# The expert layer of a graph network: tiles, order and the last two experts' output changed

## The chip, the cores and the metric

The kernel runs on one core of one Trainium2 chip. The metric is the device time of one execution in microseconds, the median of several runs. A core has a matrix engine (TensorE, in the profile PE, its weight loads PEld), a vector engine (VectorE, DVE), a scalar engine (ScalarE, ACT), GpSimd (POOL) and SyncE (SP). SP and POOL here mainly issue transfers; every transfer runs on the core's 16 DMA engines.

## What is computed

The input is 625 rows x of 1024 values, a list of 20625 edges and the weights of four layers. Each layer adds its result to x, on a layernorm of x: a gated graph layer with 8 relations, a quantized linear layer, a graph convolution, and a mixture of 8 experts. The change lies in the last one, which in the reference is, cut to what matters:

```python
logits = x @ router_w                       # 625 x 8
combine, dispatch = top2_gating(logits, capacity)
expert_in = einsum('nec,nh->ech', dispatch, x)
hmid = silu(einsum('ech,ehf->ecf', expert_in, w1) + b1)
expert_out = einsum('ecf,efh->ech', hmid, w2) + b2
y = einsum('nec,ech->nh', combine, expert_out)
out = x_before + y + 0.1 * (silu(x @ sw1 + sb1) @ sw2 + sb2)
```

Each token goes to its two best experts, an expert takes at most 196 tokens (its slots), and the two gates of a token add up to 1.

## The kernel before, in words

The graph layers take most of the time; they end with the function neighbours (L764), which adds the graph convolution to X[t] for five row tiles of 125 rows, takes the layernorm into th[t] and writes it to the DRAM table tokens. The function router makes the logits. Then VectorE finds each token's two experts and its place in each; the products positions (L883) and fill_slots (L934) turn this into token_i, which row of tokens a slot of an expert takes, and slots, which holds the slot's gate. A slot that no token takes points at spare rows past the 625th.

The shared expert's second product, shared_out (L954), comes next: per row tile and half of the columns two products, two VectorE operations onto X[t], and the finished X[t] is written to the DRAM table total (L971). This is the base of the result.

The expert loop (L982 to L1042) runs over 8 experts in pool tiles of two buffers. For each: POOL gathers the rows of its slots in two halves of 98 (L986), SP loads its row of b2, repeated on 98 partitions (L990), and its weights w1 and w2 (L993, L994, 1024 KB each); TensorE transposes the gathered rows (16 transposes in four groups, L177), ScalarE copies each group out of PSUM (L180); TensorE makes the hidden product (L1002), ScalarE the Silu (L1009); ScalarE scales b2 by the gates (L1017), TensorE makes the output product (L1022), VectorE scales it and adds the scaled b2 (L1029), and POOL adds the 98 rows into total with an indirect transfer that accumulates (L1032). An expert's two accumulating transfers wait until those of the expert before have landed, since both may hit the same row. When all have landed, SP copies total to the output (L1045).

The order on each engine is the one of the program text, moved by a scheduler where nothing forbids it; in_steps (L822) pins TensorE's steps one behind the other up to shared_out, the expert loop is not pinned. The function in_order (L110) chains transfers on SP in the order of the text. Weights live in two pools of four buffers, wts and late; w_chunk (L127) chains only those of wts. PSUM gives the products four banks (mm_tile, L105) and the transposes two.

The pools of the expert loop are opened where gated and tail were closed (L975, L976), so its tiles lie in memory that th, flat and aT held before.

Of the kernel before, what the change touches and what calls it, by code (L numbers as in the profile page):

```python
# [8 lines left out]
F32 = mybir.dt.float32  # L9
BF16 = mybir.dt.bfloat16  # L10
F32R = mybir.dt.float32r
I32 = mybir.dt.int32
# [19 lines left out]
EG = 11  # L32
BEFORE = 4096.0
NE = 8
F = 256
CAP = 196
CP = CAP // 2
# [8 lines left out]
def gnn_ffn_kernel(  # L46
# [58 lines left out]
    def mm_tile():  # L105
        return ps_mm.tile([128, HC], F32, tag="mm", name="mm")
# [17 lines left out]
        spread(queue, t, bass.AP(tensor=v.tensor, offset=v.offset, ap=[[0, P], [1, v.shape[0]]]))  # L124
        return t

    def w_chunk(pool, w, k0, c0, nk=4, cols=HC):  # L127

        t = pool.tile([128, nk, cols], F32, tag="w", name="w")
        d = nc.sync.dma_start(  # L130
            t,
            w[k0 * 128 : (k0 + nk) * 128, c0 : c0 + cols].rearrange("(k p) n -> p k n", p=128),
        )
        if pool is wts:
            in_order(d)
        return t

# [33 lines left out]
    def transposed(oT, c0, v, n, evacuate=None):  # L171

        for g in range(KD // 4):
            ps = ps_tr.tile([128, 4, 128], F32, tag="tr", name="tr")
            for k in range(4):
                f = (4 * g + k) * 128
                nc.tensor.transpose(ps[:, k, :n], v[:, f : f + 128], ident[:n, :n])  # L177
            o = oT[:, 4 * g : 4 * g + 4, c0 : c0 + n]
            if evacuate is None:
                nc.scalar.copy(o, ps[:, :, :n])  # L180
            else:
                evacuate(o, ps[:, :, :n])


    ident = const.tile([128, 128], F32, name="ident")
# [364 lines left out]
    th = []  # L550
    for t in range(NT):
        transposed(uT, t * P, X[t], P)
        th.append(gp.tile([P, D], F32, name=f"th{t}"))
        nc.scalar.activation(th[t], X[t], AF.Tanh)
        for d in spread(nc.sync, X[t], x[t * P : (t + 1) * P, :]):
            in_order(d)
# [60 lines left out]
            nc.gpsimd.tensor_add(X[t], X[t], q_bias_row)  # L617


    aT = cp.tile([P, NT, N], F32, name="aT")  # L620
    with tc.issue_after(pe_last.ins):
        for k in range(NT):
            for j0, j1 in ((0, 4), (4, NT)):
# [116 lines left out]
    def iota(t, pattern, base, channel):  # L740
        nc.gpsimd.iota(
            t,
            pattern=pattern,
            base=base,
            channel_multiplier=channel,
            allow_small_or_imprecise_dtypes=True,
        )
        return t
# [2 lines left out]
    io_cap = iota(mp.tile([P, CAP], F32, name="io_cap"), [[1, CAP]], 0, 0)  # L751
    io_tok = iota(mp.tile([P, NT, NE], F32, name="io_tok"), [[P, NT], [0, NE]], 0, 1)
    io_free = iota(mp.tile([CP, 2, NE], F32, name="io_free"), [[CP, 2], [0, NE]], N, 1)
    ones_b = mp.tile([P, P], BF16, name="ones_b")
    nc.gpsimd.tensor_copy(ones_b, ones)
    tri_b = mp.tile([P, P], BF16, name="tri_b")
# [100 lines left out]
    nc.vector.reciprocal(red, red)  # L857
    nc.vector.tensor_mul(gates, gates, wide(red))

    masks = mp.tile([P, NT, 2, NE], BF16, name="masks")  # L860
    best = [tile2("best0"), tile2("best1")]

    def argmax_mask(i, v):
# [10 lines left out]
    nc.vector.tensor_scalar(rest, masks[:, :, 0, :], -1.0, 1.0, op0=ALU.mult, op1=ALU.add)  # L874
    nc.vector.tensor_mul(rest, rest, gates)
    argmax_mask(1, rest)


    pos_tile = ps_sm.tile([128, HC], F32, tag="sm", name="pos")
    pos_ps = pos_tile[:P, : (NT + 1) * 2 * NE].rearrange("p (t c) -> p t c", t=NT + 1)  # L880
    mflat = masks.rearrange("p t i e -> p t (i e)")

    def positions(_):  # L883
        for t in range(NT + 1):
            for j in range(t):
                last = nc.tensor.matmul(
                    pos_ps[:, t, :], ones_b, mflat[:, j, :], start=(j == 0), stop=(t == NT and j == t - 1)
                )
            if t < NT:
                nc.tensor.matmul(pos_ps[:, t, :], tri_b, mflat[:, t, :], start=(t == 0), stop=True)  # L890
        return last

    in_steps(((positions, None), (shared_hidden, (0, 3 * P, N)), (shared_hidden, (1, 3 * P, N))))
    pos = mp.tile([P, NT + 1, 2, NE], F32, name="posn")
    nc.vector.tensor_copy(pos.rearrange("p t i e -> p t (i e)"), pos_ps)
    taken = mp.tile([P, 1, NE], F32, name="taken")
    nc.vector.tensor_scalar_min(taken, pos[:, NT:, 0, :], float(CAP))
    nc.vector.tensor_add(pos[:, :NT, 1, :], pos[:, :NT, 1, :], taken.to_broadcast(S3))
# [32 lines left out]
    token_i = mp.tile([CP, 2, NE], I32, name="token_i")  # L931
    free = mp.tile([CP, 2, NE], F32, name="free")

    def fill_slots(j):  # L934
        ps = ps_sm.tile([128, HC], F32, tag="sm", name="slots")
        for i in range(2):
            for t in range(NT):
                last = nc.tensor.matmul(
                    ps[:CP, : NE * 3],
                    place[:, i, t, j * CP : (j + 1) * CP],  # L940
                    brings[:, i, t, :, :].rearrange("p e v -> p (e v)"),
                    start=(i == 0 and t == 0),
                    stop=(i == 1 and t == NT - 1),
                )
        nc.vector.tensor_copy(slots[:, j].rearrange("p e v -> p (e v)"), ps[:CP, : NE * 3])
        nc.vector.tensor_scalar(free[:, j], slots[:, j, :, 0], -1.0, 1.0, op0=ALU.mult, op1=ALU.add)
        nc.vector.tensor_mul(free[:, j], free[:, j], io_free[:, j])
        nc.vector.tensor_add(token_i[:, j], free[:, j], slots[:, j, :, 1])
        return last

    sb2_row = row_tile(work, sb2, "row")
# [19 lines left out]
        base.extend(spread(nc.sync, total[t * P : (t + 1) * P, :], X[t]))  # L971
        return last

    in_steps(((fill_slots, 0), (fill_slots, 1), *((shared_out, t) for t in range(NT))))
    gated.close()  # L975
    tail.close()  # L976

    def rows_at(j, e):
        return bass.IndirectOffsetOnAxis(ap=token_i[:, j, e : e + 1], axis=0)

    sent = base + cleared
    with tc.tile_pool(name="xp", bufs=2) as xp:  # L982
        for e in range(NE):
            xe = xp.tile([CP, 2, D], F32, tag="xe", name="xe")
            for j in range(2):
                nc.gpsimd.indirect_dma_start(  # L986
                    out=xe[:, j, :], out_offset=None, in_=tokens, in_offset=rows_at(j, e)
                )
            b2_row = xp.tile([CP, D], F32, tag="b2", name="b2")
            nc.sync.dma_start(  # L990
                b2_row, bass.AP(tensor=b2.tensor, offset=b2.offset + e * D, ap=[[0, CP], [1, D]])
            )
            wa = w_chunk(wts, w1[e], 0, 0, nk=KD, cols=F)  # L993
            wz = w_chunk(late, w2[e], 0, 0, nk=2, cols=D)  # L994
            xeT = xp.tile([128, KD, CAP], F32, tag="xeT", name="xeT")
            for j in range(2):
                transposed(xeT, j * CP, xe[:, j, :], CP)
            he = xp.tile([128, 2, CAP], F32, tag="he", name="he")
            for f in range(2):
                ps = mm_tile()  # L1000
                for k in range(KD):
                    nc.tensor.matmul(  # L1002
                        ps[:, :CAP],
                        wa[:, k, f * 128 : (f + 1) * 128],
                        xeT[:, k, :],
                        start=(k == 0),
                        stop=(k == KD - 1),
                    )
                nc.scalar.activation(  # L1009
                    he[:, f, :], ps[:, :CAP], AF.Silu, bias=b1_sb[:, e, f : f + 1]  # L1010
                )
            ye = xp.tile([CP, 2, D], F32, tag="ye", name="ye")
            earlier, sent = sent, []
            for j in range(2):
                gate_of = slots[:, j, e, 2:3]
                b2g = work.tile([P, D], F32, tag="xn", name="xn")[:CP, :]
                nc.scalar.mul(b2g, b2_row, gate_of)  # L1017
                for h in range(2):
                    hs = slice(h * HC, (h + 1) * HC)
                    ps = mm_tile()  # L1020
                    for f in range(2):
                        nc.tensor.matmul(  # L1022
                            ps[:CP, :],
                            he[:, f, j * CP : (j + 1) * CP],
                            wz[:, f, hs],
                            start=(f == 0),
                            stop=(f == 1),
                        )
                    nc.vector.scalar_tensor_tensor(  # L1029
                        ye[:, j, hs], ps[:CP, :], gate_of, b2g[:, hs], op0=ALU.mult, op1=ALU.add  # L1030
                    )
                d = nc.gpsimd.indirect_dma_start(  # L1032
                    out=total,
                    out_offset=rows_at(j, e),
                    in_=ye[:, j, :],
                    in_offset=None,
                    compute_op=ALU.add,
                )
                for other in sent:
                    tc.declare_no_dep(d.ins, other.ins, reason="a token has one slot of an expert")  # L1040
                after(d, earlier)
                sent.append(d)  # L1042

    flat_out = [v.rearrange("n d -> (n d)").rearrange("(a b) -> a b", a=80) for v in (out, total[:N, :])]
    after(nc.sync.dma_start(*flat_out), sent)  # L1045


# ---- launch: one core; inputs in the reference's types, weights that are contracted over their
# [39 lines left out]
```

## Time and profile before

| What | Value |
|---|---|
| median of 3 runs | 1367.83 us (1367.31 to 1372.51) |
| profiled execution, its own time | 1372.71 us |
| its span on the profile's clock | 1371.0 us |
| TensorE busy | 1302.0 us, 95% |
| VectorE, ScalarE, GpSimd busy | 604.8, 183.4, 511.1 us |
| DMA moved | 178.79 MB, mean 130 GB/s |
| hidden products of the experts, L1002, 256 records | 46.5 us |
| output products of the experts, L1022, 128 records | 56.2 us |
| slot numbers ready (last token_i) | 1200.5 us |
| shared product on TensorE | 1199.55 to 1216.96 us |
| last expert's product ends | about 1352.4 us |

[...] The chain of waits follows the work that ended last back to what released it. The windows give busy time per engine, then the clock granted to TensorE (1.00 is full), then the mean busy share of the DMA engines and what they moved.

### The profile page before, as it was taken

How to read it: one execution, taken by the hardware profiler on the slowest of the kernel's cores; microseconds unless marked ns; L12 is line 12 of the kernel's file. 1: busy time of each engine (PE TensorE's matmuls, PEld its weight loads, DVE VectorE, ACT ScalarE, POOL GpSimd, SP SyncE). 2: the span in 40 equal slices, each digit the busy share in tenths (PEclk: the TensorE clock that was granted, in tenths of full speed). 3: DMA queues.
4: the chain of work that ended last, by engine and by line, in shares of the span. 5: the costliest groups of instructions: out<-in, count | busy, mean ns of one | idle time of the engine just before them, and what ended most of it. 6: DMA issues, size and time to landing. Idle time of an engine off the chain costs nothing. (4 is left out here: it accounts for less than half of the span.)

```text
span 1371.0 us, 10587 instructions
## 1 busy us (share of the span) xinstructions
PE 1302.0 (95%) x4050; PEld 693.5 (51%) x4050; DVE 604.8 (44%) x1042; ACT 183.4 (13%) x335; POOL 511.1 (37%) x262
## 2 busy tenths in 40 slices
PE   6999999999999999999999999899989999969994
PEld 3444444444444444444777777444445445736652
DVE  6942555555555555001555564423358214441121
ACT  1000000000000000001212211300011111212231
POOL 2016888888888888751200000313100000013221
PEclk9999999999999999999999999999999999989997
DMA  8994445545544443349999722412040231168955
GB/s 252 271 248 119 112 110 122 122 113 122 126 110 120 83 92 73 63 96 236 181 235 226 186 70 94 138 47 93 0 138 15 77 123 49 46 187 233 271 96 122
DMA packets 140155, 178.79 MB, mean 130 GB/s; under 512 B 74758, under 2 KB 91517, under 8 KB 137536
## 3 DMA queue, kind: packets, MB, share of 16 engines
q1 hardware_dynamic: 55998, 126.65, 31.9%
q0 software_dynamic: 79968, 36.12, 17.3%
q10 hardware_dynamic: 4134, 15.29, 3.0%
q8 instruction: 34, 0.56, 0.2%
q14 instruction: 21, 0.17, 0.0%
HBM read 139.04 MB, written 41.18 MB: 131 GB/s over the span
## 5 line engine op out<-in xcount | busy, mean ns | idle before, releaser
L224 PE MATMUL mm<-w,xT 128*125 128x512 f32 x1440 | 622.3, 595 | 1.0 <-ACT xT L180 1.0
L363 POOL DMA_INDIRECT table<-hits,idx x165 | 401.6, 2434 | 138.5 <-issue 68.0
L224 PEld LDWEIGHTS mm<-w,xT 128*125 128x125 f32 x1440 | 270.8, 188 | 348.1 <-issue 345.7
L343 DVE SCALAR_TENSOR_TENSOR junk<-kr,key,wm 125x1375 f32<-125x1375 f32 x165 | 272.4, 1651 | 202.1 <-DMA kr<-key_rows 198.2
L432 PE MATMUL mm<-lo,b 125*125 125x512 f32 x400 | 160.9, 402 | 1.9 <-DVE lo L489 1.9
L432 PE MATMUL mm<-hi,b 125*125 125x512 f32 x400 | 159.5, 399 | 0.0
L388 ACT COPY y<-mm 125x512 f32<-125x512 f32 x80 | 46.8, 585 | 544.2 <-PE mm L224 544.2
L986 POOL DMA_INDIRECT xe<-tokens,token_i x16 | 16.1, 1006 | 226.6 <-DMA total<-X 213.2
L446 DVE SCALAR_TENSOR_TENSOR X<-mm,rc,X 125x512 f32<-125x512 f32 x80 | 60.0, 750 | 76.5 <-PE mm L432 76.3
L432 PEld LDWEIGHTS mm<-lo,b 125*125 125x125 f32 x400 | 75.1, 188 | 22.5 <-DVE lo L489 3.8
L432 PEld LDWEIGHTS mm<-hi,b 125*125 125x125 f32 x400 | 75.0, 188 | 18.0
L571 PE MATMUL mm<-w,xT 128*125 128x512 f32 x160 | 73.2, 603 | 0.0
L1029 DVE SCALAR_TENSOR_TENSOR ye<-mm,slots,xn 98x512 f32<-98x512 f32 x32 | 24.0, 751 | 110.8 <-PE mm L1022 110.8
L695 PE MATMUL mm<-w,xT 128*125 128x512 f32 x160 | 70.0, 595 | 1.6 <-ACT xT L180 1.6
L571 PE MATMUL mm<-w,flat 128*125 128x512 f32 x160 | 70.3, 592 | 0.0
L487 ACT CAST hi<-y 125x512 fp32r<-125x512 f32 x80 | 43.3, 617 | 159.4 <-PE mm L432 159.4
L465 POOL DMA_DIRECT2D btot<-table x16 | 17.7, 1157 | 111.5 <-DMA btot<-table 108.9
L1022 PE MATMUL mm<-w,he 128*98 128x512 f32 x128 | 56.2, 592 | 0.0
L1032 POOL DMA_INDIRECT total<-ye,token_i x16 | 24.7, 1541 | 83.2 <-DVE ye L1029 83.2
L426 DVE TENSOR_SCALAR crow<-cn 1x376 f32<-1x376 f32 (+1 forms) x16 | 7.4, 465 | 106.2 <-PE cn L423 106.2
L489 DVE TENSOR_TENSOR lo<-y,hi 125x512 fp32r<-125x512 f32 x80 | 51.4, 681 | 5.4 <-ACT hi L487 5.4
L1002 PE MATMUL mm<-xeT,w 128*128 128x196 f32 x256 | 46.5, 342 | 6.0 <-ACT xeT L180 6.0
(168 smaller groups left out, 842.1 us busy)
## 6 DMA issues: line engine op xcount, KB each, us to landing
w<-in_L_gnn_weight_dram SPq DMA_DIRECT2D x32, 1024.0 KB
w<-in_L_ffn_w_dram SPq DMA_DIRECT2D x16, 1024.0 KB
table<-zero SPq DMA_DIRECT2D x4, 3054.0 KB
yd<-y ACTq DMA_DIRECT2D x10, 1120.0 KB
y<-yd SPq DMA_DIRECT2D x10, 1120.0 KB
b<-table SPq DMA_DIRECT2D x8, 1367.2 KB
btot<-table POOLq DMA_DIRECT2D x8, 1367.2 KB, 19.1
kr<-key_rows POOLq DMA_DIRECT2D x15, 671.4 KB, 9.3
```

The costliest lines, as they stand in the source:

```text
L224: last = nc.tensor.matmul(ps[:P, :], xT[:, k, t * P : (t + 1) * P], ch[k // 4][:, k % 4, :], start=(k == 0), stop=(k == KD - 1),)
L343: d = nc.vector.scalar_tensor_tensor(junk, kr, key[:, c : c + 1], wm[:, (EG - 1 - j) * P : (2 * EG - 1 - j) * P], op0=ALU.is_equal, op1=AL ...
L363: d = nc.gpsimd.indirect_dma_start(out=table, out_offset=bass.IndirectOffsetOnAxis(ap=idx[:, c : c + 1], axis=0), in_=hits[:, c : c + 1], ...
L388: evac = nc.scalar.copy(y[:, t, :], ps)
L432: last = nc.tensor.matmul(ps[:P, :], lhs, part, start=(k == 0 and part is y[k][0]), stop=(k == NT - 1 and part is y[k][-1]),)
L446: added = nc.vector.scalar_tensor_tensor(X[t][:, hs], ps[:P, :], rc[:, r, t : t + 1], X[t][:, hs], op0=ALU.mult, op1=ALU.add,)
L487: behind(nc.scalar.copy(hi, y[:, k, :]), act_last)
L489: nc.vector.tensor_sub(lo, y[:, k, :], hi.bitcast(F32))
L571: last = nc.tensor.matmul(ps[:P, :], lhs[:, k % KD, ts], gate_w[h][k // 4][:, k % 4, :], start=(k == 0), stop=(k == 2 * KD - 1),)
L695: last = nc.tensor.matmul(ps[:P, :], xT[:, k, t * P : (t + 1) * P], gcn_w[h][k // 4][:, k % 4, :], start=(k == 0), stop=(k == KD - 1),)
L1002: nc.tensor.matmul(ps[:, :CAP], wa[:, k, f * 128 : (f + 1) * 128], xeT[:, k, :], start=(k == 0), stop=(k == KD - 1),)
L1022: nc.tensor.matmul(ps[:CP, :], he[:, f, j * CP : (j + 1) * CP], wz[:, f, hs], start=(f == 0), stop=(f == 1),)
```

## The change

Eight experts as before, with the same products. What differs:

- Expert tiles lie in memory that is idle by then: the gathered rows in th0 to th3 (two experts), the transposed rows in flat, the expert output and b2 in the first three quarters of aT (even experts) and btot (odd experts), the Silu's output in th4. No pools are opened.
- All steps of TensorE are pinned: transposes of expert e+1, turn(e + 1), stand between the hidden product and the output product of expert e.
- POOL issues the gathers of experts 0 and 1 ahead of everything, those of e+2 after the hidden product of e in the text.
- b2, w1 and w2 of an expert are chained on SP in this order (chain=True).
- For experts 6 and 7 a second set of row numbers, out_i, is made: a free slot points not at a spare row but at a token that is not routed to this expert (it adds zero there). These two experts accumulate straight into the output, after total has been copied to it; the copy waits for experts 0 to 5. The row numbers need two more columns in the positions (others), ten comparisons on VectorE (find_others) and 20 small bf16 products among the shared ones (fill_others).

```diff
+NL = 2
-    def w_chunk(pool, w, k0, c0, nk=4, cols=HC):
+    def w_chunk(pool, w, k0, c0, nk=4, cols=HC, chain=False):
...
-        if pool is wts:
+        if pool is wts or chain:
             in_order(d)
...
+    nc.vector.tensor_add(others, masks[:, :, 0, NE - NL :], masks[:, :, 1, NE - NL :])
+    nc.vector.tensor_scalar(others, others, -1.0, 1.0, op0=ALU.mult, op1=ALU.add)
...
+    def find_others():
+
+        nc.vector.tensor_scalar(before, others, -float(N), float(N), op0=ALU.mult, op1=ALU.add)
+        nc.vector.tensor_add(before, before, pos_all[:, :NT, 2 * NE :])
+        for e in range(NL):
+            for t in range(NT):
+                d = nc.vector.tensor_scalar(
+                    spots[:, e, t, :], io_cap, before[:, t, e : e + 1], None, op0=ALU.is_equal
+                )
+                behind(d, numbered[-1])
...
-    in_steps(((fill_slots, 0), (fill_slots, 1), *((shared_out, t) for t in range(NT))))
-    gated.close()
-    tail.close()
...
+    in_steps(((fill_slots, 0), (fill_slots, 1)))
+    find_others()
+    in_steps(((shared_out, 0), (shared_out, 1), (fill_others, None), *((shared_out, t) for t in range(2, NT))))
+
+    tiles = {
+        "xeT": [flat[:, c : c + KD * CAP].rearrange("p (k c) -> p k c", k=KD) for c in (2 * N, 2 * N + KD * CAP)],
+        "ye": [v[:CP, : 2 * D].rearrange("p (j d) -> p j d", j=2) for v in (aT_flat, btot_flat)],
+        "b2": [v[:CP, 2 * D : 3 * D] for v in (aT_flat, btot_flat)],
+        "he": [th_flat[:, c : c + 2 * CAP].rearrange("p (f c) -> p f c", f=2) for c in (0, HC)],
+    }
...
+    def load_expert(e):
+        b2_row = tiles["b2"][e % 2]
+        in_order(
+            nc.sync.dma_start(
                 b2_row, bass.AP(tensor=b2.tensor, offset=b2.offset + e * D, ap=[[0, CP], [1, D]])
             )
+        )
+        weights[e] = (
+            w_chunk(wts, w1[e], 0, 0, nk=KD, cols=F),
+            w_chunk(late, w2[e], 0, 0, nk=2, cols=D, chain=True),
+        )
...
+            d = nc.gpsimd.indirect_dma_start(
+                out=(total if e < NE - NL else out),
+                out_offset=rows_at(j, e, e >= NE - NL),
+                in_=ye[:, j, :],
+                in_offset=None,
+                compute_op=ALU.add,
+            )
+            for o in sent:
+                tc.declare_no_dep(d.ins, o.ins, reason="a token has one slot of an expert")
+            after(d, earlier)
+            sent.append(d)
+        return last
+
+    gather(0)
+    load_expert(0)
+    gather(1)
+    in_steps(((turn, 0),))
+    for e in range(NE):
+        for n in range(NE - NL, NE) if e == NE - NL else (e + 1,):
+            if n < NE and n not in weights:
+                load_expert(n)
+        if e == NE - NL:
+            d = in_order(nc.sync.dma_start(flat_rows(out), flat_rows(total)))
+            after(d, sent)
+            sent = [d]
+        in_steps(((expert_hidden, e),))
+        if e + 2 < NE:
+            gather(e + 2)
+        in_steps((*(((turn, e + 1),) if e + 1 < NE else ()), (expert_out, e)))
+    tail.close()
```

The functions gather, turn, expert_hidden and expert_out hold the same operations as the loop body before, taken apart. Built, the program's order on POOL is: gathers of experts 0 to 3, the scatter of 0, gather of 4, scatter of 1, gather of 5, and so on to gather 7, then the scatters of 4 to 7. On SP, b2 of expert 0 and its w1 stand ahead of the last write of tokens, its w2 right behind that; b2 of expert 1 stands among the writes of total, its weights behind the last of these; then b2, w1, w2 of experts 2 to 7, then the copy of total to the output.

## The prediction

> **What bounds the kernel now.** I read the page's 40 slices first, then the chain of waits from 1050 us on, then the timeline of the last 170 us and its windows. All times are on the profiled execution's clock.
>
> ```profile
> PE   6999999999999999999999999899989999969994
> PEclk9999999999999999999999999999999999989997
> DMA  8994445545544443349999722412040231168955
> ```
>
> TensorE is full almost everywhere; two exceptions lie in the changed part, slice 36 (1199.6 to 1233.9 us), where the granted clock dips too, and the last one. The change touches nothing ahead of 1180 us except what is loaded when, so the question is these two holes and the DMA row beside them. The chain of waits, in order of time, with start, length and who:
>
> ```profile
> 1215.37 2.47 DMA total<-X
> 1217.84 0.02 issue
> 1217.86 1.49 POOL xe L986
> 1219.34 0.30 issue
> 1219.65 10.63 DMA xe<-tokens,token_i
> 1230.28 0.14 issue
> 1230.41 1.54 PE tr L177 x8
> 1231.95 7.45 PE mm L1002 x32
> ...
> 1248.99 5.57 PE mm L1002 x32
> 1254.57 6.87 PE mm L1022 x16
> 1261.43 0.35 PE tr L177 x4
> ```
>
> TensorE ends the shared product at 1216.96 and has nothing until expert 0's rows land: the gather is held until the shared result has been written to total. The hole costs twice, since expert 0 then takes 7.45 us for what later takes 5.57. From expert 1 on, the distance from one L1002 to the next is 15.17 us, of which 5.57 + 6.87 = 12.44 are products. The tail is in the timeline, the load of the DMA engines in the windows (the last two columns are DMA share and GB/s):
>
> ```profile
> 1353.69 1.52 POOL L1032 DMA_INDIRECT total<-ye,token_i  x1 [2.10 <-DVE ye L1029]
> 1359.68 0.60 SPq L1045 DMA_DIRECT2D out_dram<-total  x1
> ```
> ```profile
> 1250.00:1260.00 10.00, 10.00 (x42) 6.56 (x41) 1.68 (x3) 1.97 (x3) 2.11 (x3) 1.00 1.00 254
> 1260.00:1270.00 10.00, 8.90 (x54) 7.42 (x52) 1.32 (x2) 3.36 (x8) 4.14 (x4) 1.00 1.06 288
> 1270.00:1280.00 10.00, 8.90 (x36) 4.52 (x35) 3.00 (x4) 4.02 (x7) 3.55 (x3) 1.00 1.04 260
> 1280.00:1290.00 10.00, 10.00 (x43) 6.83 (x42) 1.50 (x2) 1.65 (x3) 2.09 (x3) 1.00 1.01 269
> 1290.00:1300.00 10.00, 8.90 (x54) 7.42 (x53) 1.50 (x2) 3.45 (x7) 4.49 (x4) 1.00 1.05 283
> ```
>
> So the last product ends at 1352.42, the last scatter lands near 1359.5, and the copy to the output takes until about 1369.4. And for 50 us the DMA engines are full, at (254+288+260+269+283)/5 = 271 GB/s, while TensorE just does not notice.
>
> **The start of the experts.** The gathers now write into th0 to th3, free since the tokens went out near 1176. They need only the slot numbers (token_i, done at 1200.5), not the shared result. Four gathers follow at once on POOL. A gather took 0.94 to 1.49 us there; beside a busy VectorE the nearest row is the table scatter L363 at 2.43. Expert 0's two rows land at the worst at 1200.6 + 2 x 2.43 + 7.1 (the shortest issue-to-landing of a gather, since the engines are near empty) = 1212.6, ahead of need either way. Between the shared products come 20 small bf16 products (fill_others); the 20 of L886/L890 took 1.12 us, the slot products L938 0.085 us a record, so between 1.1 and 1.7 us, and I take 1.2. The shared product ends at 1218.2. Expert 0's transposes then need four groups with a ScalarE copy each: 0.43 + 4 x 0.46 = 2.3 us. Expert 0's L1002 begins at 1220.5 instead of 1231.95: **11.45 us gained**. Without the hole the clock stays at 1.00 (it was 0.61 in 1220 to 1230), so expert 0 also takes the later period.
>
> **The period.** The new order is hidden(e), transposes of e+1, out(e). In the old one, from 1261.43 to 1264.16, 2.73 us passed between output product and next hidden product, with one 1.16 us scaling of b2 on ScalarE between the copies. Now the transposes' stall is PSUM alone (two banks, four groups): 0.43 + 0.1 + 0.46 (copy of group 1, after the 0.42 us Silu, which runs beside group 1), then 0.43 and 0.43: 1.85 us. And out(e) no longer waits 0.51 us for the Silu. Period: 5.57 + 1.85 + 6.87 = 14.3. Bounds: 14.0 (16 unstalled transposes, 16 x 0.1) and 15.2 (nothing gained). Expert 0 gains 17.04 - 14.3 = 2.74, experts 1 to 6 gain 0.87 each, 5.2; expert 7 has no transposes to hide its Silu, -0.5. Sum 7.4. TensorE ends at 1352.42 - 11.45 - 7.4 = **1333.5**.
>
> **The tail.** The copy moves ahead of the last two experts, which add into the output itself. After the last product remain 0.76 (VectorE), POOL's issue and 5.8 us to landing: 1352.42 to 1359.5 before, then 1.6 us to the span's end as now: 8.7 in place of 18.6 us, **9.9 us gained** if the copy is hidden. All together 28.8 us: span 1342.2.
>
> **What costs nothing, and its cover.** Two more VectorE operations ahead of the positions (0.2 us each): masks were ready at 1187.78, TensorE came at 1188.33; if that cover is short, 0.2 us. Ten is_equal operations (0.25 each) ahead of the shared additions: TensorE has four PSUM banks, 6.9 us of cover against 2.5. Two columns more in the position products and two iotas on an idle POOL: nothing. b2's scaling now sits ahead of Silu on ScalarE and waits for VectorE's last ye of the expert before: done about 2.0 us into hidden(e), Silu is due at 2.8; if late, 0.4 us an expert.
>
> **What the change takes away: early loads.** The diff chains b2, w1, w2 of each expert on SP. Before, w1 of experts 0 to 3 and w2 of 0 to 2 were issued by 1196.3. Now b2 of expert 0 lies in aT, read by the neighbour products until 1171, and stands ahead of its weights; b2 of expert 1 lies in btot and waits for fill_others (about 1208), and its weights stand behind the last write of total (1219.6). From expert 2 on b2 waits for ScalarE's scaling of b2 of expert e-2, about 2 us into hidden(e-2), so weights are asked for 26.7 us ahead of use. Three w1 and two w2 of 1024 KB, 5.2 MB, move into the full stretch. The ledger from 1219.6: rest of total<-X 0.9 MB, seven pairs of weights 14.7, six b2 rows (392 KB) 2.4, six gathers and six scatters (98 x 2 rows of 4 KB, 0.80 each) 9.6: 27.6 MB. At 271 GB/s that is 102 us, to 1321.5. One expert is 2.1 + 0.4 + 0.8 + 0.8 = 4.1 MB, 15.2 us against a period of 14.3.
>
> [...] The row of this kernel, 271 GB/s with gathers and accumulating scatters among the loads, is the measured mix; it decides. The scatter alone explains much: in 1330 to 1340, where little else runs, the windows show a share of 0.25 for 40 GB/s, so 2.5 us of all engines for 0.4 MB.
>
> With 271 GB/s the weights still arrive: w2 of expert 7 is ahead of the last scatter in the ledger and due at 1326.6. Late is the tail. Scatter 5 is ready at 1307.5; on empty engines it lands at 1313.3, at the ledger's end at 1321.5. The copy follows (0.6 issue and 9.1 landing now, alone), then scatter 6 (second half issued 1.8 later, 5.8 to land) and scatter 7 behind it: copy's landing + 0.2 + 7.6 + 0.2 + 7.6 + 1.6 = +17.2. SP has nothing queued behind the copy; on POOL only scatter 7 stands behind scatter 6. From 1313.3: 1323 + 17.2 = 1340.2, less than TensorE's 1342.2, nothing lost. From 1321.5: 1331.2 + 17.2 = 1348.4, 6.2 lost. POOL's queue shares the engines with SP's, so scatter 5 need not wait for all; I take two thirds of it, 4 us lost: span 1346, 25 us below 1371.0. The profiled execution took 1372.71, 1.7 more than its span and 4.9 more than the median 1367.83; 1367.83 - 25 = **1343**.
>
> **Rivals.** (a) All hidden: 28.8 us, 1339. For it: the engines idle from 1180 to 1200, and two experts' rows are fetched early. Against: share 1.00 to 1.06 for 50 us. (b) The mix runs slower. Priced one by one from windows where each ran with little else, an expert takes 6.7 us of all engines for its weights (two w1 in 1072 to 1084 at 291 GB/s, w2 and its like in 1108 to 1124 at 339), 1.3 for b2, about 3.6 for the gather (1308 to 1320) and 5.1 for the scatter: 16.7 us for 4.1 MB, 246 GB/s. 27.6 MB then take 112 us, to 1331.5; w2 of expert 7 (due 1326.6) is a few us late, the copy lands at 1341.2: span 1358.4, time 1355. For it: windows of 218 to 225 GB/s wherever scatters fall; against it: the same mix kept 271 for 50 us. (c) Slower than before: the same place, the serial end (copy, scatter 6, scatter 7). It decides from a copy landing at 1371.0 - 17.2 = 1353.8; less 9.7 for the copy, the ledger would have to take 124.5 us, 222 GB/s held throughout. At 215 GB/s it ends at 1348, copy 1357.7, span 1375: 1372. Only single 3 us windows are that low. (d) The transposes gain nothing (period 15.2) but the ends do: six times 0.9, 5 to 6 us less gained; with slower demand the DMA engines keep up, so 1345, inside the main case.
>
> **How the numbers follow.** Main case with (d) 45%, 1340 to 1349; (a) 30%; (b) 20%; (c) 5%. The range goes from 1336 (all hidden and a period of 14.0, 2 us, with 1 us of scatter between runs) to 1358 (case (b) with the same spread). A measurement of this kernel can tell about 0.5%, 6.8 us, from no change: faster than 1361 holds (a), the main case and nearly all of (b), 0.92; within is the rest of (b) and the start of (c), 0.04; slower 0.04.
>
> **What would show it.** Right: no TensorE hole after the shared product and a clock of 1.00 there; L1002 to L1002 near 14.3; DMA share about 1 from 1220 to 1320; the chain ending with copy, scatter 6, scatter 7. (a) is shown by a chain that ends TensorE, VectorE, scatter 7; (b) by TensorE waiting for DMA w or for th. Wrong would be a gather landing after 1218, or a period still at 15.

## The result and the profile after

| | before | after |
|---|---|---|
| median of 5 runs | 1369.92 us (1367.31 to 1372.51) | 1357.57 us (1356.07 to 1360.88) |
| span of the profiled execution | 1371.0 us | 1358.7 us |
| from the end of the slot products to the span's end, below "the stage" | 171.3 us | 157.6 us |

The ratio is 0.9917, with a 95% interval of 0.9893 to 0.994: 12.3 us faster at the medians, where 25 were forecast. That is inside the stated range, but hardly half of the gain, and within 3 us of what rival (b) gave (1355, span 1358.4). The slot products are the last TensorE work that the change leaves where it was; in the profiled executions they end up to 9 us apart (1192.6 to 1201.8 us), so below the stage behind them is compared, and times by their ratios.

The rows of the 40 slices first (of the page of the kernel after):

```profile
PE   6999999999999999999999999899998999999894
PEclk9999999999999999999999989899998999999897
DMA  8994444444544533339999740711040011349995
```

The hole at the shared product is gone: the slices from 1189 to 1257 us read 9 on both TensorE rows. New is the 8 on both in the slice from 1257 to 1291: that is what has to be explained. DMA reads 9 in the three slices from 1223 us to 1325. The chain of waits of the kernel after:

```profile
1208.06 0.88 PE others L989 x20
1208.93 10.40 PE mm L1013 x24
1219.34 0.35 PE tr L178 x4
...
1221.38 2.95 PE mm L1078 x16
...
1225.47 26.15 DMA w<-in_L_ffn_w_dram
1251.61 0.14 issue
1251.75 5.57 PE mm L1078 x32
...
1258.04 26.41 DMA w<-in_L_ffn_w_dram
1284.45 0.14 issue
1284.58 7.78 PE mm L1078 x32
...
1308.28 6.87 PE mm L1104 x16
...
1322.34 6.87 PE mm L1104 x16
```

Expert 0's hidden product (now L1078) follows the shared product 2.0 us later, the wait of ten us is gone, and once nothing starves it the period is 1322.34 - 1308.28 = 14.06 us. But two of the chain's pieces are weights: w1 of expert 2 and of expert 4, each landing 26 us after it was asked for. The waits view of TensorE in the stage adds them up (us in total, times, longest):

```profile
PE mm L1078 <- DMA w<-in_L_ffn_w_dram: 6.4, 2, 4.5
```

And the same windows as before, of the kernel after (clock, DMA share, GB/s last):

```profile
1250.00:1260.00 10.00, 8.01 (x51) 7.28 (x52) 0.63 (x1) 3.66 (x7) 2.95 (x3) 1.00 1.06 267
1260.00:1270.00 10.00, 10.00 (x40) 6.33 (x39) 3.00 (x4) 2.72 (x3) 3.67 (x3) 1.00 1.05 274
1270.00:1280.00 10.00, 9.76 (x41) 5.09 (x39) 2.25 (x3) 3.24 (x6) 3.52 (x3) 1.00 1.07 271
1280.00:1290.00 10.00, 5.53 (x20) 5.45 (x20) 0.75 (x1) 1.43 (x2) 1.54 (x1) 0.66 1.06 255
1290.00:1300.00 10.00, 9.76 (x45) 5.89 (x44) 2.05 (x3) 3.38 (x7) 3.24 (x3) 1.00 1.05 272
```

DMA is as full as before, at 255 to 274 GB/s (before: 254 to 288), but now TensorE notices: it is busy for 5.53 of 10 us in 1280 to 1290. The wait there costs twice. The mean clock of that window falls to 0.66, and the product of 32 records behind it (two to each of its 16 matmuls) takes 7.78 instead of 5.57 us. Within the wait of 4.5 us the clock averages 0.75 (1280.0 to 1284.5), behind it 0.50 (1284.5 to 1288.0) and 0.88 (1288.0 to 1292.4). The wait of 1.9 us at 1250 left it at 1.00 (1249.8 to 1257.4). Last the tail, in the timeline of POOL and SP of the kernel after:

```profile
1313.78 1.51 POOL L1114 DMA_INDIRECT total<-btot,token_i  x1 [10.06 <-DMA total<-aT,token_i]
1316.23 1.53 POOL L1114 DMA_INDIRECT total<-btot,token_i  x1 [0.94 <-DVE btot L1111]
1326.56 0.61 SPq L1136 DMA_DIRECT2D out_dram<-total  x1
1337.53 1.52 POOL L1114 DMA_INDIRECT out_dram<-aT,out_i  x1 [19.78 <-DVE btot L1111]
1339.36 1.53 POOL L1114 DMA_INDIRECT out_dram<-aT,out_i  x1 [0.30 <-issue]
1346.97 1.52 POOL L1114 DMA_INDIRECT out_dram<-btot,out_i  x1 [6.08 <-DMA out_dram<-aT,out_i]
```

The scatter of expert 5 (btot, to total) goes at 1313.78, after 10.06 us of waiting for the one of expert 4, and with its second half at 1316.23. It lands ten us later, the copy follows at 1326.56 and lands near 1336.7, then come the scatters of experts 6 and 7, one behind the other, to the span's end. The releaser named for 1337.53 is VectorE at work on expert 7 (btot); its work for expert 6 (aT) was long done. What came then was the copy, and other runs below name it.

So two readings stood after the result. **Theory A**: the DMA engines are the bound; the 5.2 MB of loads that the change moved from the idle stretch into the full one took back half of what its three parts gain. **Theory B**: POOL's queue and the chain of scatters are the bound, whatever SP loads. Later **theory C**: not the bytes, but the chain on SP as such holds the weights.

### The profile page after: what moved, and what is told of

Same layout as the page of the kernel before. It is cut to its first block, busy times and chain, and to the rows that moved or that the text cites. A ratio compares the mean times of both kernels' runs of the same rounds, so it can differ in the third digit from the quotient of the medians.

```text
span 1358.7 us, 10658 instructions
## 1 busy us (share of the span) xinstructions
PE 1301.9 (96%) x4070; PEld 693.4 (51%) x4070; DVE 608.3 (45%) x1061; ACT 184.6 (14%) x335; POOL 515.2 (38%) x264
## 2 busy tenths in 40 slices
DMA packets 140156, 178.79 MB, mean 132 GB/s; under 512 B 74759, under 2 KB 91518, under 8 KB 137537
## 3 DMA queue, kind: packets, MB, share of 16 engines
q0 software_dynamic: 79968, 36.12, 17.3%
## 5 line engine op out<-in xcount | busy, mean ns | idle before, releaser
L1062 POOL DMA_INDIRECT th<-tokens,token_i x16 | 19.0, 1185 | 238.0 <-DVE btot L978 196.2
L1104 PE MATMUL mm<-w,th 128*98 128x512 f32 x128 | 56.3, 592 | 0.0
L1078 PE MATMUL mm<-flat,w 128*128 128x196 f32 x256 | 46.4, 340 | 6.6 <-DMA w<-in_L_ffn_w_dram 6.4
L1078 PEld LDWEIGHTS mm<-flat,w 128*128 128x128 f32 x256 | 45.0, 197 | 10.9 <-issue 10.5
```

The costliest lines, as they stand in the source:

```text
L1078: last = nc.tensor.matmul(ps[:, :CAP], weights[e][0][:, k, f * 128 : (f + 1) * 128], tiles["xeT"][e % 2][:, k, :], start=(k == 0), stop=(k ...
L1104: last = nc.tensor.matmul(ps[:CP, :], he[:, f, j * CP : (j + 1) * CP], weights[e][1][:, f, hs], start=(f == 0), stop=(f == 1),)
```

## Experiments

All ratios are to the kernel before on the same chip. Ratios times 1370 us give the gains in us.

| kernel | median us | ratio (95%) | stage us | TensorE waits for w |
|---|---|---|---|---|
| after | 1357.57 | 0.9917 (0.9893 to 0.994) | 157.6 | 6.4 us, 2 |
| e1: b2 and w2 not chained | 1343.61 | 0.98 (0.9775 to 0.9826) | 144.0 | none |
| e9: b2 alone not chained | 1344.55 | 0.9799 (0.9777 to 0.982) | 144.4 | none |
| e2: weights of one expert only | 1345.3 | 0.9805 (0.9783 to 0.9826) | 143.4 | none |
| e10: after, w1 in rows of 8 KB | 1353.83 | 0.988 (0.9859 to 0.9901) | 152.9 | none |
| e5: e1 with 4.6 MB put back | 1358.85 | 0.9918 (0.9896 to 0.9941) | 161.7 | none |
| e3: after, copy last | 1356.8 | 0.9906 (0.9882 to 0.9929) | 161.5 | 9.0 us, 3 |
| e4: after, transposes late | 1354.95 | 0.9873 (0.9849 to 0.9897) | 157.2 | none |
| e6: e1, transposes late | 1349.01 | 0.9843 (0.9824 to 0.9863) | 149.5 | none |
| e7: e1, copy last | 1350.86 | 0.9859 (0.9839 to 0.988) | 152.3 | none |
| e8: e1, transposes late and copy last | 1357.57 | 0.9916 (0.9898 to 0.9935) | 157.6 | none |

**The loads early again (e1).** b2 and w2 leave SP's chain, as before the change; everything else of it stays.

```diff
-        in_order(
-            nc.sync.dma_start(
-                b2_row, ...
-            )
-        )
+        nc.sync.dma_start(b2_row, ...)
-            w_chunk(late, w2[e], 0, 0, nk=2, cols=D, chain=True),
+            w_chunk(late, w2[e], 0, 0, nk=2, cols=D),
```

> One part undone: b2 and w2 are no longer chained on SP, so w1 of experts 0 to 3 and w2 of 0 to 2 are asked for before 1200 us again; all else as changed. Theory A (the 5.2 MB that the chain moved into the experts' stretch fill the DMA engines, starve TensorE and make the copy late): the ledger falls from 27.6 to 22.4 MB, 83 us at 271 GB/s, so the engines are full only until about 1303; no wait of TensorE for w; TensorE ends near 1332, the copy lands near 1325, time about 1344. Theory B (gathers and accumulating scatters on POOL's queue are what slows everything, whatever SP loads): TensorE's waits shrink but scatters still take 10 us to land, the copy lands after 1332, time about 1352.

Measured 1343.61, what theory A gave. Seven weights are asked for before the last write of total, as in the kernel before, where the change has two. TensorE waits for no weight, and the DMA engines are relieved sooner. Windows of this run:

```profile
1270.00:1280.00 10.00, 9.76 (x56) 7.86 (x55) 1.50 (x2) 4.08 (x8) 4.40 (x4) 1.00 1.06 271
1280.00:1290.00 10.00, 10.00 (x40) 6.44 (x39) 3.00 (x4) 2.72 (x3) 3.51 (x3) 1.00 0.98 233
1290.00:1300.00 10.00, 9.76 (x42) 5.33 (x41) 2.25 (x3) 3.24 (x6) 1.51 (x1) 1.00 0.39 86
```

The share falls to 0.39 at 1290, where the kernel after had 1.04 until 1310 and 1.03 until 1320; some 6 us of that are the earlier slot products of this execution. And the tail, in the timelines of SP, POOL and VectorE of this run:

```profile
1306.85 0.60 SPq L1134 DMA_DIRECT2D out_dram<-total  x1
1317.59 1.52 POOL L1112 DMA_INDIRECT out_dram<-aT,out_i  x1 [15.02 <-DMA out_dram<-total]
1319.41 1.52 POOL L1112 DMA_INDIRECT out_dram<-aT,out_i  x1 [0.30 <-issue]
1322.84 0.75 DVE L1109 SCALAR_TENSOR_TENSOR btot<-mm,slots,xn 98x512 f32<-98x512 f32 x1 [0.97 <-PE mm L1102]
1327.03 1.51 POOL L1112 DMA_INDIRECT out_dram<-btot,out_i  x1 [6.09 <-DVE btot L1109]
```

The copy goes at 1306.85, 13.5 us before that of the kernel after as counted from the slot products. The last row names VectorE, but the first half of scatter 7 needs only the first two of its four operations for expert 7, and the second of them (1322.84) was done at 1323.59. The half went 3.4 us later than that, and 7.62 us after the second half of scatter 6; in the kernel after that distance is 7.61 us, and there the landing of scatter 6 is named. So the copy, scatter 6 and scatter 7 set the end here too, by little: with VectorE alone to wait for, the second half could have gone at about 1327.3 instead of 1328.85 (an estimate from these rows).

**The weights of one expert only (e2).** It leaves out the loads of w1 and w2 of experts 1 to 7; all experts use those of expert 0.

```diff
     def load_expert(e):
...
+        if e > 0:
+            weights[e] = weights[0]
+            return
```

> Leaves out the loads of w1 and w2 of experts 1 to 7: all experts use those of expert 0. The ledger falls to 12.9 MB. Theory A: share of the DMA engines well under 1 after 1225, gathers land in about 7 us and scatters in about 6, TensorE ends near 1332, copy lands near 1323, time about 1343; this is the most that freeing the loads can bring. Theory B: scatters still take about 10 us and the time stays above 1348.

Measured 1345.3, with a share of 0.54 to 0.72 in 1220 to 1300. Nearly 15 MB less bring nothing beyond e1: once the DMA engines are off the path, relieving them further is worth nothing. POOL's transfers are the same here as in the kernel after, so they alone are not what held it. Theory B fell.

**The parts undone, with the change's loads (e3, e4).** In e3 all experts add into total and the copy comes last; in e4 the transposes of expert e+1 come behind the output product of e.

```diff
-                out=(total if e < NE - NL else out),
-                out_offset=rows_at(j, e, e >= NE - NL),
+                out=total,
+                out_offset=rows_at(j, e),
...
+    after(in_order(nc.sync.dma_start(flat_rows(out), flat_rows(total))), sent)
```

```diff
-        in_steps((*(((turn, e + 1),) if e + 1 < NE else ()), (expert_out, e)))
+        in_steps(((expert_out, e), *(((turn, e + 1),) if e + 1 < NE else ())))
```

> One part undone: experts 6 and 7 add into total like the others, and the copy to the output comes last; the second set of row numbers is still made. Theory A: TensorE ends where it does now, 1341, and then need 18.6 us as before the change: span 1360, time about 1359, so the early copy brought 1 to 2 us where 9.9 were forecast. If the early copy brings its 9.9 us in full, the time is 1367.

> One part undone: the transposes of expert e+1 stand behind the output product of expert e instead of ahead of it. Theory A: the DMA engines set the pace, so what the order costs on TensorE (about 0.9 us an expert) only shortens its waits for w: 1356 to 1360. If TensorE sets the pace, 6 us more than with the change, 1363 to 1364.

Neither is slower than the kernel after: 1356.8 and 1354.95. Both parts are there in the traces and bring nothing that these medians can tell as long as the DMA engines set the pace. (The one profiled stage of e3 is 3.9 us longer than that of the kernel after, with 9.0 us of waits, so zero holds to a few us only.) In e4 the period is 15.19, so that weights are asked for at longer distances, and TensorE waits for none; but the chain of waits of e4 ends in scatters:

```profile
1285.51 13.14 DMA total<-btot,token_i
...
1302.58 12.55 DMA total<-aT,token_i
...
1317.82 7.12 DMA total<-btot,token_i
1324.99 10.42 DMA out_dram<-total
```

A scatter that landed after 5.8 us before takes 13.14 and 12.55 us here from the issue of its second half, and each scatter waits for the one before it. The end comes from the full DMA engines, through late weights in e3 and late scatters in e4.

**The parts undone, with the loads early (e6, e7, e8).** The same two edits on e1, apart and together. e8 keeps, of the three parts, only the early start.

> As e1_loads_free, with the transposes of expert e+1 behind the output product of e. With the DMA engines relieved TensorE sets the pace, so the order must now pay what it was forecast to: seven times (15.2 - 14.07), 8 us: 1351. If the order is worth nothing either way, 1344.

> As e1_loads_free, with experts 6 and 7 adding into total and the copy last. From TensorE's end 18.6 us remain instead of the 12.7 in e1_loads_free: 1349 to 1350. If the early copy had been worth the 9.9 forecast, 1353; if it is worth nothing, as with the change's own loads, 1344.

> As e1_loads_free with both the order of the transposes and the early copy undone, so that only the early gathers into idle tiles are left: 1343.6 + 8 + 6 = 1357 to 1358, 12 to 13 us below before, of which 11.5 are the hole on TensorE and 1 to 2 the slower clock behind it.

Now each part has a price. The early start alone: 0.9916, 11.5 us. The order of the transposes: 0.9859 against e8's 0.9916, and 0.98 against e6's 0.9843, 7.8 and 5.9 us. The early copy: 0.9843 against 0.9916, and 0.98 against 0.9859, 10.0 and 8.1 us. Together, in e1, 27.4 us. Each ratio has an interval of 0.2% either way, about 3 us, so these prices hold to some 4 us. The kernel after gains what e8 gains: it paid the order and the copy back in full.

**Bytes or chain (e5, e9).** e5 puts the amount back without the chain: ten loads of 448 KB that nothing reads, behind the last write of total.

```diff
+    for again in range(10):
+        t = again % NT
+        after(nc.sync.dma_start(X[t][:P16, :], w2[again % NE][: 2 * P16 // 2, :]), base)
```

> As e1_loads_free (loads early again), with ten loads of 448 KB, 4.6 MB, that nobody reads put behind the last write of total, so that the experts' stretch moves nearly as much as with the change while every weight of experts 0 to 3 but one is there early. Theory A (the amount): 17 us more of full engines, of which the 9 us that they were free from 1290 to 1307 take part; scatters 4 and 5 land late again, the copy lands 5 to 10 us later than in e1_loads_free: 1348 to 1354. Theory C (it is the chaining of weights behind b2 and the late asking, the amount is harmless): as e1_loads_free, 1343 to 1345.

Measured 1358.85: what e1 gains over the kernel after is gone again, so bytes in the full stretch are enough to lose it. The loss is larger than the forecast (1348 to 1354), and no weight is late. The chain of waits of e5 shows what is:

```profile
1255.15 21.73 DMA aT<-in_L_ffn_b_dram
...
1278.04 1.13 ACT xn L1097
1279.17 0.62 ACT th L1083 x2
1279.80 0.38 ACT flat L181
1280.18 0.04 issue
1280.23 0.94 PE tr L178 x8
1281.17 3.45 PE mm L1102 x8
```

and its waits view, for TensorE:

```profile
PE tr L178 <- ACT flat L181: 16.9, 8, 12.7
```

A row of b2, that of expert 4, took 21.73 us to land. It was asked for at 1255.15, where e1 asks at 1245.76, since SP stood 11.99 us in issuing a weight ahead of it. ScalarE's scaling of b2 (xn L1097) stands ahead of the Silu and of the copies of the transposes, so TensorE stood 16.9 us in all, 12.7 of them at one place, before PSUM banks that ScalarE had not emptied (2.0 us in the kernel after). The prediction priced a late scaling at 0.4 us an expert; that price does not hold when a load is what makes it late. So e5 loses by another way than the kernel after, and what it shows is that the amount is enough, not that it works through the weights.

e9 does the opposite: only b2 leaves the chain, w1 and w2 stay in it.

> The changed kernel with only b2 taken out of SP's chain; w1 and w2 stay chained behind each other. The amount that is moved stays, the head of the chain goes: w1 and w2 of experts 0 and 1 and w1 of 2 can then be issued before the last tokens are written, so about 4 of the 5.2 MB return to the empty stretch. Theory A (bytes moved into the full stretch are what the change lost by): TensorE no longer waits for a w, 1344 to 1348 us. Theory C (the chain's order as such, weights held behind each other's issue): the w1 and w2 still stand in one chain, so most of the loss stays, 1353 to 1358 us.

Measured 1344.55, as e1, and TensorE waits for no weight. The tile rows of w on SP (count, then shortest, median and longest ns of the issuing instruction, first and last start), after 1195 us, of the kernel after and of e9:

```profile
L131 SPq DMA_DIRECT2D w<-in_L_ffn_w_dram x14: 367/2444/12416, 1221.6 to 1306.8; - x14
```
```profile
L131 SPq DMA_DIRECT2D w<-in_L_ffn_w_dram x11: 367/368/1025, 1196.8 to 1277.0; - x11
```

Of 16 weights the kernel after asks for 14 behind the last write of total; in e9 11 are left after 1195, two of them by 1202, so nine behind that write, as in e1. The last is asked for at 1277 instead of 1307. A chain on SP does no harm as such (theory C fell); b2 at its head does, since it waits for a tile that is in use. The end of e9 is again copy, scatter 6, scatter 7, and here the row of scatter 7 says so:

```profile
1333.12 1.52 POOL L1112 DMA_INDIRECT out_dram<-btot,out_i  x1 [6.12 <-DMA out_dram<-aT,out_i]
```

**Cheaper bytes (e10).** On the kernel after: a partition takes one run of 8 KB of w1 instead of eight runs of 1 KB, and the transposes take every eighth column; the sums are the same with their terms in another order.

```diff
+    def w1_chunk(e):
+        w = wts.tile([128, KD, F], F32, tag="w", name="w")
+        in_order(nc.sync.dma_start(w, w1[e].rearrange("(p k) n -> p k n", k=KD)))
+        return w
...
+            v = rows_of_slots(e, j).rearrange("n (p k) -> n k p", k=KD)
...
+                    last = nc.tensor.transpose(ps[:, k, :CP], v[:, 4 * g + k, :], ident[:CP, :CP])
```

> The changed kernel with w1 loaded so that a partition takes one run of 8 KB instead of eight runs of 1 KB (row p*8+k of w1 to partition p, and the transposes take every eighth column, so the hidden product sums the same terms in another order). Theory A: the DMA engines are the bound, so cheaper bytes help as fewer bytes do: seven w1 at 339 instead of 291 GB/s save 7 x 0.5 = 3.6 us of all engines, 2 to 5 us faster than the changed kernel, 1352 to 1356. If the row length costs nothing in the mix, or the strided transposes cost TensorE more, no change or slower: 1357 to 1360.

Measured 1353.83, 0.988 against 0.9917: some 5 us by the ratios, though the intervals touch (to 0.9901, from 0.9893). The five windows of 20 us from 1220 to 1320 average (259 + 287 + 291 + 272 + 254) / 5 = 273 GB/s, those of the kernel after (243 + 273 + 272 + 263 + 262) / 5 = 263. TensorE waits for no weight, although the transposes cost it 17.3 instead of 14.3 us in all. The same bytes in fewer pieces end the waits as fewer bytes do, for part of the gain. SP shows something else, in its tile rows of this run:

```profile
L1050 SPq DMA_DIRECT2D w<-in_L_ffn_w_dram x7: 341/375/1132, 1219.9 to 1294.3; - x7
L131 SPq DMA_DIRECT2D w<-in_L_ffn_w_dram x7: 378/426/873, 1220.9 to 1294.7; - x7
```

No issue takes longer than 1.13 us, where with short pieces one took 12.42. It asks sooner, too: w1 of expert 4 goes to the queue 26.0 us before its product starts, in the kernel after 22.1 us before it is needed. How much of the gain comes from the rate and how much from asking sooner, this run does not separate.

## Why the prediction was off, step by step

**The three parts: right.** With the loads early they give 27.4 us (e1), where 28.8 was the sum with all hidden. The start: from the end of the slot products to expert 0's hidden product 20.3 us, forecast 20.8; fill_others 0.88 us, forecast 1.2; the clock 1.00 (1200 to 1222). Expert 0's gathers on POOL took 2.90 and 2.01 us, with VectorE busy for 5.83 of the 6 us from 1201 (the row taken for the upper end was 2.43) and landed in time. The period: 14.06, forecast 14.3 with a lower bound of 14.0. The early copy: 8.1 to 10.0, forecast 9.9. Rival (d) fell.

**The ledger: right as a sum.** 27.6 MB at 271 GB/s were to end at 1321.5; the engines were full until about 1323 (a share of 1.03 in 1320 to 1323, 0.45 in 1323 to 1326).

**The step that failed: "With 271 GB/s the weights still arrive: w2 of expert 7 is ahead of the last scatter in the ledger and due at 1326.6."** It tests the last load against the end of the sum, and no load on the way: how long a load takes to land is nowhere set against how long ahead it is asked for. Forecast was a lead of 26.7 us. w1 of expert 2 was asked for at 1225.47, 24.4 us before TensorE was ready for it, and landed 26.15 us later; w1 of expert 4 was asked for at 1258.04, 22.1 us before, and landed 26.41 us later. The differences, with the 0.14 us of issue behind each, are the two waits of 1.9 and 4.5 us.

Why 26 us: the prediction itself had 15.2 us of transfers an expert against a period of 14.3, so that what is asked for piles up from 1220 on. Between 1219.6 and 1251.6, when w1 of expert 2 landed, the engines moved 8.3 MB (32 us at 258 GB/s). Asked for up to 1238.5 were the last 0.9 MB of total, four weights of experts 1 and 2 (4.2), a row of b2 (0.4), gathers 2 and 3 (1.6) and scatter 0 (0.8), 7.9 MB; another 4 MB were asked for before it landed. So it landed when about as much had moved as had been asked for up to 1238.5. This sum is an estimate.

The runs show that b2 at the head of the chain is what lost the time (e9), that relieved engines end the waits (e1, e2), and that bytes alone lose it again (e5, through b2). They do not part the amount from the lead: e1 and e9 change both (in e9 the last weight is asked for 47 us before its product, in the kernel after 28), and no run keeps the short lead with 5 MB less in the full stretch.

**What it cost, against the forecast span of 1346.** TensorE waited 6.4 us and ran 2.2 us longer on a slow clock: its end came at 1341.4 instead of 1333.5. Scatter 5 was therefore ready at 1316.2 instead of 1307.5, behind most of the ledger, and still took 10.1 us to land instead of 5.8. The copy landed at 1336.7, where "two thirds of it" meant 1328.8: 7.9 us. (1.4 us of each of the three shifts on the clock are the slot products, which in this execution ended at 1201.1 instead of 1199.7; for the copy 6.5 us are left.)

**A second term was too small by itself: the serial end of 17.2 us.** It took 1358.7 - 1336.7 = 22.0 us: the two gaps 0.8 and 0.9 instead of 0.2 each, scatter 6 8.6 instead of 7.6, the last scatter to the span's end 11.7 instead of 9.2. That is 4.8 us, and 7.9 + 4.8 is the 12.7 us by which the span was missed. The moved loads have no part in these 4.8: from the first half of scatter 6 to the span's end the kernel after takes 21.2 us, e1 21.4 and e9 20.9, with all weights landed before that in each.

**The two thirds** was a guess between 1313.3 and 1321.5 on how POOL's transfers share with SP's. Here they do share: scatter 5 landed 10.1 us after the issue of its second half (in e4 scatters took 12.55 and 13.14) while a weight took 26. But each of these scatters landed late, and every scatter waits for the one before it, so the lateness adds up along that chain (the scatters in e4's lines) instead of being paid once.

**The rivals.** (b) came within 3 us for the time, and its signs came: TensorE waiting for w, the copy late. Its reason did not hold: it had the mix at 246 GB/s with the ledger ending at 1331.5, and the mix kept 263. (a) is what e1 and e9 come to in time, 27.4 and 27.5 us, but not in its sign: both end with copy, scatter 6, scatter 7. (c) did not come near: the copy landed 17 us ahead of the point at which the prediction has it decide.

**Why scatters 6 and 7 land later than the 5.8 us forecast.** Little else runs then (from 1337.5 to 1346 the DMA share is 0.58, scatter 6 included), and two things differ from the scatters before: they add into the output, and their halves follow each other by 1.8 us instead of 3.4. Three second halves on engines that are not full, in e9 of scatter 5 and scatter 6 (share 0.64 in 1302 to 1318, 0.45 in 1318 to 1334), in e7 of scatter 6 (0.40 in 1320 to 1326, 0.47 in 1326 to 1332), tell them apart:

```profile
1306.21 6.47 DMA total<-btot,token_i
...
1325.47 6.75 DMA out_dram<-aT,out_i
```
```profile
1324.80 5.51 DMA total<-aT,token_i
```

With halves 1.86 us apart the one into total takes 6.47 us, nearly the 6.75 of the one into the output (1.82 apart); with halves 3.43 us apart it takes 5.51. So the nearness of the halves is most of it, as far as one execution of each shows.

**What stays open.** Amount and lead, as said above. And what is left beyond e1 and e9, which beat the change by 16 us: their end is the chain of copy, scatter 6 and scatter 7, in e1 only about 1.5 us later than TensorE and VectorE alone would allow, and no version with a shorter chain was run.

## What to carry to other kernels

When a change moves loads into a stretch where the DMA engines are already full, it is not enough that the total fits by the end: keep the ledger as a running sum and hold every load, and every transfer that others are chained behind, against its own due time. Before ordering transfers behind each other on a queue, ask what the first of them waits for: here a row of 392 KB that waited for its tile kept 5 MB of weights out of an idle stretch, and taking it out of the chain more than doubled the gain. And undo parts both with and without the suspected bottleneck: with it, undoing the order or the copy cost nothing that could be told from zero; without it, 6 and 8 us.

## What the runs showed of the hardware that was not expected

SP's issuing instruction can itself stand. In the kernel after, w2 of expert 2, asked for behind b2 and w1, held SP for 12.42 us, as the timeline shows:

```profile
1226.06 12.42 SPq L131 DMA_DIRECT2D w<-in_L_ffn_w_dram  x1
```

The shortest of the kernel after took 0.37 us; in the kernel before one took 0.39 us at 1196.34, with a DMA share of 0.12 (1194 to 1198). With w1 in eight times fewer pieces (e10, 132988 packets in all instead of 140156) the longest was 1.13 us, with the engines as full (a share of 1.01 to 1.04 from 1220 to 1300) and the same bytes. With the short pieces but more weights asked for early, in the kernel before and in e1, it was 0.81 and 1.34 us. So the bytes alone do not set it; what does, no run shows. While SP stands there, b2 of the next expert is not asked for either: that of expert 3 went at 1238.58, right behind.
